# Softmax denominators summed on GpSimd in one buffer, seven PSUM banks, and values multiplied in halves, in an attention and LoRA-mixture layer

## The chip, the cores and the metric

The kernel runs on one core of a Trainium2 chip. The metric is the device time of one execution in microseconds (us); lower is better. All data is float32 unless said otherwise.

## The reference

One transformer layer on `x` of shape 2 × 2048 × 512 (two sequences), in two halves, each with a residual:

```python
x = x + attention(layernorm(x))      # 16 heads of 32, rotary q and k, causal softmax, Wo
x = x + ffn(layernorm(x))            # base linear + bias, and top-2 of 8 LoRA experts of rank 16

# attention, per head
scores = q @ k.T / sqrt(32); scores[above the diagonal] = -inf
attn   = softmax(scores); ctx = attn @ v; out = ctx @ Wo.T

# ffn, per token
probs = softmax(x @ router_w.T + router_b); gate = the two largest, divided by their sum
y     = x @ base_w.T + base_b + 2 * sum over experts of gate[e] * (x @ A[e]) @ B[e]
```

## The kernel before

**Blocks and steps.** The 4096 tokens are cut into eight blocks of 512, four for each sequence: block n is the j-th of its sequence, j = n mod 4. A block has four steps (n, g), one for each group g of four heads, since four heads of 32 fill the 128 partitions. Step (n, g) attends 512 queries to 4j+4 key tiles of 128 keys each. The last four tiles lie on the diagonal; of these, tile 4j+1 and 4j+3 share one buffer, because together they are 512 wide (384 and 128), and tile 4j+2 has 256 columns.

**The two passes over the scores.** `row_maxima` computes scores with the queries on the partitions (`sm`, L367), takes each row's maximum on VectorE (`pm`, L375 and L380) and leaves minus the maximum, split into three bf16 parts, in `max`. `attend` computes the scores again, transposed, with the keys on the partitions (`sc`, L463), adds the shift by a small bf16 matmul (L471), and ScalarE takes the exponential from PSUM into an SBUF buffer `pt` of 128 × 4 × 512 (L485): for one key tile the weights of four heads and 512 queries. On the diagonal GpSimd sets the weights above it to zero (`affine_select`, L494).

**Values and denominators.** `weighted` multiplies the weights of a key tile by its values and adds up in the PSUM bank `av` (L519), four heads side by side. When both tiles of a pair are multiplied, GpSimd adds the second one's weights to the first's in place (L534), two heads at a time, and `summed` later adds the pair's weights over the keys by a matmul with `ones` into the PSUM bank `den` (L545), again four heads side by side. After a step's last pair ScalarE copies `den` to `sum`; its four rows go to DRAM and come back spread over 128 partitions (`few`), VectorE takes the reciprocal, and they go back over DRAM, repeated over 32 partitions each (`sum<-over`). GpSimd then multiplies the context by it (L581). The last step takes the reciprocal directly.

**The order.** TensorE, ScalarE and VectorE run in the order in which the program writes their instructions. GpSimd's and SP's instructions are placed by the scheduler. `side_by_side` interleaves one step's maxima with the former step's weights. It gives out phases: in each, two heads' `sm` and the other two heads' `sc` run side by side on TensorE. Between phases the main loop puts other work:

- `between()` does what is due of `due`: `weighted` two phases after its exponentials, `summed` three after its pair;
- a planner takes projections (`kps`, `qps`, `vps`, L185 and L210) and the stages of the last block but one's second half (`ops`, `mid`, `yps`, L239, L265, L320) from `waiting`, by their times and a credit;
- `ahead()` takes a `summed` one phase early where nothing else was given to a phase.

**Buffers.** The PSUM banks of scores and projections are six, taken in turn (`bank`); `av` and `den` have one each, eight in all. `pt` has four buffers in turn (`PTS`). Before a tile's exponentials `before()` does every entry of `due` that still holds the buffer to be reused. All weights are loaded once, at the start, and stay in SBUF: `wq`, `wk`, `wv`, `wo` and `base_w` are 1 MB each. `wo` is used by `ops` alone and `base_w` by `yps` alone.

Of the kernel before, what the change touches and what calls it, by code (L numbers as in the profile page):

```python
# [9 lines left out]
F32 = mybir.dt.float32  # L10
# [16 lines left out]
LORA_SCALING = 32.0 / 16.0  # L27
THETA = 10000.0
MASKED = -1e30
PTS = 4  # L30
SWAP = [i ^ 1 for i in range(32)]


# [1 line left out]
def preln_attention_moe_lora(  # L35
# [33 lines left out]

    def bank(name, shape=(P, BLK), dtype=F32):  # L70
        banks[0] += 1
        return ps.tile(list(shape), dtype, tag=f"ps{banks[0] % 6}", name=name)


    ident = const.tile([P, P], F32, name="ident")
# [48 lines left out]
    wq = load_weight(wq_t, "wq")  # L124
    first_turn = load_turn(0)
    wv = load_weight(wv_t, "wv")
    wo = load_weight(wo_t, "wo")
    exp_in = load_weight(expert_in, "exp_in")
    bias_sb = const.tile([P, D + E], F32, name="bias_sb")
    nc.sync.dma_start(out=bias_sb, in_=bias.to_broadcast([P, D + E]))  # L130
    base_w = load_weight(base_wt, "base_w")
    exp_out = const.tile([ER, D], F32, name="exp_out")
    nc.sync.dma_start(out=exp_out, in_=expert_out)

    def moments(xt, t, name):

# [90 lines left out]
    def finish(n, ctx_t):  # L227
# [3 lines left out]

        def load(t):
            held["x"].append(load_x(n, t, True))

        def output(t):
            xt = held["x"][t]
            po = bank(f"ops_{n}_{t}")
            for c in range(NC):
                nc.tensor.matmul(  # L239
                    out=po,  # L240
                    lhsT=ctx_t[c][:, bass.ts(t, P)],
                    rhs=wo[:, c, :],
                    start=(c == 0),
                    stop=(c == NC - 1),
                )
            nc.vector.tensor_add(xt, po, xt)
            held["by"].append(moments(xt, t, f"f{n}"))

# [67 lines left out]
        def result(t):  # L316
            xt = held["x"][t]
            po = bank(f"yps_{n}_{t}")
            for c in range(NC):
                nc.tensor.matmul(  # L320
                    out=po,
                    lhsT=held["xn_t"][:, c, bass.ts(t, P)],
                    rhs=base_w[:, c, :],
                    start=(c == 0),
                    stop=False,
                )
# [83 lines left out]
    due = []  # L410
    phase, begun = [0], [0]

    def later(phases, tile, do, early=0):
        due.append((phase[0] + phases, tile, do, early))
        due.sort(key=lambda entry: entry[0])

    def between():

        many = sum(entry[0] <= phase[0] for entry in due)
        many = min(many, 1 + many // 3)  # L420
        for _ in range(many):
            due.pop(0)[2]()
        return many > 0

    def ahead():

        for i, entry in enumerate(due):
            if entry[0] - entry[3] <= phase[0]:
                return due.pop(i)[2]()


    def attend(s):

# [3 lines left out]
        tiles = NT * (j + 1)  # L437
        together = [(kt,) for kt in range(diagonal + 1)]
        together += [(diagonal + 1, diagonal + 3), (diagonal + 2,)]
        pts, index, paired = {}, {}, {}  # L440

        def low(kt):
            return max(kt - diagonal, 0) * P
# [7 lines left out]
        def quad(*kts):  # L451

            all_of = slice(0 if len(kts) > 1 else low(kts[0]), BLK)
            sc = {}

            def take(r):
                sc[r] = bank(f"sc_{n}_{g}_{kts[0]}_{r}")

            def scores(i, r):
                if i < len(kts):  # L460
                    jj, tt = divmod(kts[i], NT)
                    rows = slice(DK * r, DK * r + DK)
# [12 lines left out]

            def weigh(r):
                if kts[0] not in pts:
                    pt = p2.tile(
                        [P, 4, BLK], F32, tag="pt", bufs=PTS, name=f"pt_{n}_{g}_{kts[0]}"
                    )  # L480
                    for kt in kts:
                        index[kt], pts[kt] = begun[0], pt
                    begun[0] += 1
                pt = pts[kts[0]]
                nc.scalar.activation(  # L485
                    pt[:, r, all_of], sc[r][:, all_of], AF.Exp, scale=1.0 / math.sqrt(DK)
                )
                if kts[0] >= diagonal and r % 2:

                    at = all_of.start  # L490
                    on = pt[:, r - 1 : r + 1, at : at + len(kts) * P]
                    if len(kts) > 1:
                        on = on.rearrange("p h (k q) -> p h k q", q=P)
                    nc.gpsimd.affine_select(  # L494
                        out=on, in_=on, compare_op=ALU.is_ge, fill=0.0, base=0,
                        pattern=[[0, 2]] + [[0, len(kts)]] * (len(kts) > 1) + [[1, P]],
                        channel_multiplier=-1,
                    )

            def before():  # L500

                while any(tile <= begun[0] - PTS for _, tile, _, _ in due):
                    due.pop(0)[2]()

            def after():

                oldest = diagonal + 1 if kts[0] == tiles - 2 else kts[0] - kts[0] % 2
                later(2, index[oldest], lambda: weighted(kts))

            return before, take, scores, shift, weigh, after  # L510

        def weighted(kts):
            if kts[0] == 0:
                s["av"] = ps_o.tile([P, BLK], F32, tag="av", name=f"av_{n}_{g}")
            for kt in kts:
                jj, tt = divmod(kt, NT)
                for r in range(4):
                    rows = slice(DK * r, DK * r + DK)
                    nc.tensor.matmul(  # L519
                        out=s["av"][rows, low(kt) :],  # L520
                        lhsT=values[jj][g][:, tt, rows],
                        rhs=pts[kt][:, r, place(kt)],
                        start=(kt == 0),
                        stop=(kt == tiles - 2),
                    )

            for kt in kts:
                kt -= kt % 2
                paired[kt] = paired.get(kt, 0) + 1
                if paired[kt] == 2:  # L530
                    lo = low(kt + 1)
                    for r in (0, 2):
                        some = pts[kt][:, r : r + 2, place(kt, lo)]
                        nc.gpsimd.tensor_add(some, some, pts[kt + 1][:, r : r + 2, place(kt + 1)])  # L534
                    later(3, index[kt], lambda kt=kt: summed(kt), 1)
            if kts[-1] == tiles - 2:
                s["dest"] = wide.tile([P, BLK], F32, tag="ctx", bufs=6, name=f"ctx_{n}_{g}")
                nc.scalar.copy(s["dest"], s["av"])

        def summed(kt):  # L540
            lo = low(kt)
            if kt == 0:
                s["den"] = ps_o.tile([P, BLK], F32, tag="den", name=f"den_{n}_{g}")
            for r in range(4):
                nc.tensor.matmul(  # L545
                    out=s["den"][DK * r : DK * r + DK, lo:],
                    lhsT=ones,
                    rhs=pts[kt][:, r, lo:],
                    start=(kt == 0),
                    stop=(kt == tiles - 2),  # L550
                )
            if kt == tiles - 2:
                total = p2.tile([P, BLK], F32, tag="tmp", bufs=5, name=f"sum_{n}_{g}")
                nc.scalar.copy(total, s["den"])
# [155 lines left out]
    for step in steps + [None]:  # L710
# [18 lines left out]
        for i in range(slots):  # L729
# [3 lines left out]
            for _ in side_by_side(*todo):  # L733
# [14 lines left out]
                while waiting and waiting[0][2] <= phase[0]:  # L748
# [13 lines left out]
                if not given:  # L762
                    ahead()
        late = part(weights, slots - 1, slots)
        if step:
            split()
# [2 lines left out]
        phase[0] += 1  # L769
        between()  # L770
    while due:
        due.pop(0)[2]()
    while aside:
        aside.pop(0)[1]()
    for stage in finish(len(blocks) - 1, contexts[len(blocks) - 1]):
# [52 lines left out]
```

## Time and profile before

| what | us |
|---|---|
| median of three runs | 1982.68 (1980.56 to 1984.05) |
| profiled execution, time | 1982.82 |
| profiled execution, span from first to last instruction | 1981.0 |
| TensorE (PE) busy | 1918.0, 97% of the span |
| GpSimd (POOL) busy | 1008.7, 51% |
| VectorE (DVE) busy | 1018.2, 51% |
| ScalarE (ACT) busy | 768.0, 39% |
| the adds of L534 on GpSimd | 609.9 in 320 instructions |
| `den` matmuls, L545 | 163.3 in 1280 instructions, two for each f32 matmul |
| mean granted TensorE clock | 0.987 |

A row of the costliest groups gives line, engine, operation, result and operands, shape and count; then, behind the first bar, the group's busy time and the mean of one in ns; behind the second, the time for which the engine stood before them and what ended most of it. Matmuls of four heads run side by side, so the busy time of a group is less than count times mean. Blocks are long or short by j; by the first scores of each block's first step the blocks begin at about 68, 177, 388, 669, 1000, 1126, 1365 and 1644, and from 1940 on only the last block's second half is left.

### The profile page before, as it was taken

What the parts mean: (1) busy time and instruction counts of PE and PEld (TensorE: products, weight loads), DVE (VectorE), ACT (ScalarE), POOL (GpSimd) and SP (SyncE); (2) the same over time, 40 slices, a digit from 0 to 9 for tenths busy, and PEclk for the clock granted to TensorE, in tenths of its full rate; (3) what the DMA queues carried; (4) which work ended last, traced back from release to release, by engine and by line L of the source; (5) the groups of instructions that cost most, each with busy time, mean ns of one, the idle gap of its engine ahead of it and who ended that gap; (6) DMA issues with size and microseconds to landing.
All of it is one profiled execution on the core that took longest, in us unless ns stands there. A gap on an engine that the chain in (4) does not pass through costs nothing.

```text
span 1981.0 us, 31399 instructions
## 1 busy us (share of the span) xinstructions
PE 1918.0 (97%) x12256; PEld 731.2 (37%) x12256; DVE 1018.2 (51%) x2760; ACT 768.0 (39%) x1601; POOL 1008.7 (51%) x906
## 2 busy tenths in 40 slices
PE   7999999999999999999999999999999999999997
PEld 3433433333333333333343434333433333333333
DVE  3555555555554655553255546446565555555403
ACT  1323342344433444353532334224434334443451
POOL 3545554455464555355565345435555545553572
PEclk9999999999999999999999999989999999999999
DMA  5000110000100000100000001100011000001000
GB/s 186 23 12 13 32 35 22 7 7 28 60 1 7 7 1 18 48 23 8 10 28 12 28 28 38 49 7 7 2 38 49 1 6 7 1 7 44 6 7 22
DMA packets 34861, 46.33 MB, mean 23 GB/s; under 512 B 12956, under 2 KB 13468, under 8 KB 34712
## 3 DMA queue, kind: packets, MB, share of 16 engines
q1 hardware_dynamic: 34712, 44.32, 7.0%
q8 instruction: 96, 1.57, 0.3%
q14 instruction: 53, 0.43, 0.1%
HBM read 35.40 MB, written 8.90 MB: 22 GB/s over the span
## 4 chain that ended last, share of the span: by engine, by line
PE 83%; POOL 7%; issue 4%; DVE 4%; ACT 1%; DMA 1%; SPq 0%; POOLq 0%; DVEq 0%
PE sm L367 24%; PE av L519 13%; PE den L545 6%; PE ops L239 6%; PE vps L210 6%; PE qps L185 5%; PE kps L185 5%; PE yps L320 5%; PE sc L471 5%; PE sc L463 4%; POOL pt L534 3%; POOL pt L494 2%; PE mid L265 1%; PE yps L327 1%; ACT pt L485 1%
## 5 line engine op out<-in xcount | busy, mean ns | idle before, releaser
L485 ACT ACTIVATE pt<-sc 128x512 f32<-128x512 f32 (+1 forms) x1152 | 595.1, 572 | 950.8 <-PE sc L471 882.0
L534 POOL TENSOR_TENSOR pt<-pt,pt 128x1024 f32<-128x1024 f32 (+2 forms) x320 | 609.9, 1920 | 339.2 <-ACT pt L485 193.6
L463 PE MATMUL sc<-q,k 32*128 32x512 f32 (+3 forms) x2560 | 677.5, 576 | 10.7 <-DVE parts L392 10.1
L367 PE MATMUL sm<-k,q 32*128 32x512 f32 (+3 forms) x2560 | 644.1, 574 | 6.3 <-POOL q L201 3.6
L380 DVE TENSOR_REDUCE pm<-sm 128x1 f32<-128x512 f32 x768 | 490.8, 685 | 286.5 <-PE sm L367 273.6
L367 PEld LDWEIGHTS sm<-k,q 32*128 32x128 f32 x2560 | 221.4, 184 | 375.0 <-issue 148.7
L519 PE MATMUL av<-pt,v 128*32 128x512 f32 (+3 forms) x2560 | 306.0, 550 | 19.1 <-POOL pt L494 14.2
L375 DVE CUSTOM_DVE_ANT_0 sm<-sm,mask 128x128 f32<-128x128 f32 (+3 forms) x512 | 245.8, 512 | 141.8 <-PE sm L367 118.7
L471 PE MATMUL sc<-max,ones_b 3*128 3x512 bf16 (+3 forms) x1280 | 261.2, 346 | 0.0
L463 PEld LDWEIGHTS sc<-q,k 32*128 32x128 f32 x2560 | 233.1, 185 | 51.2 <-issue 24.2
L494 POOL TENSOR_SCALAR_AFFINE_SELECT pt<-pt 128x256 f32<-128x256 f32 (+1 forms) x192 | 93.0, 485 | 154.7 <-ACT pt L485 152.2
L545 PE MATMUL den<-pt,ones 128*32 128x512 f32 (+1 forms) x1280 | 163.3, 569 | 0.0
L519 PEld LDWEIGHTS av<-pt,v 128*32 128x32 f32 x2560 | 57.5, 109 | 201.5 <-issue 142.1
L185 PE MATMUL kps<-xnt_a,wk 128*128 128x512 f32 x256 | 123.3, 626 | 5.0 <-ACT xnt_a L156 4.9
L239 PE MATMUL ops<-wo,ctx 128*128 128x512 f32 x256 | 120.2, 614 | 2.7 <-POOL ctx L581 2.7
L320 PE MATMUL yps<-base_w,xnt_f 128*128 128x512 f32 x256 | 116.9, 599 | 2.6 <-DVE pm L380 1.6
L185 PE MATMUL qps<-xnt_a,wq 128*128 128x512 f32 x256 | 118.3, 605 | 0.0
L210 PE MATMUL vps<-wv,xnt_a 128*128 128x512 f32 x256 | 117.5, 604 | 0.0
L471 PEld LDWEIGHTS <-ones_b 3*128 3x128 bf16 x1280 | 78.3, 94 | 101.0 <-issue 94.5
L200 POOL TENSOR_TENSOR sw_q<-sw_q,sin 128x512 f32<-128x512 f32 x32 | 40.7, 1273 | 112.5 <-DVE sw_q L198 112.5
L200 POOL TENSOR_TENSOR sw_k<-sw_k,sin 128x512 f32<-128x512 f32 x32 | 40.7, 1273 | 109.2 <-DVE sw_k L198 93.8
L581 POOL TENSOR_TENSOR ctx<-ctx,sum 128x512 f32<-128x512 f32 x32 | 40.6, 1268 | 90.1 <-DMA sum<-over 84.8
(85 smaller groups left out, 1246.4 us busy)
## 6 DMA issues: line engine op xcount, KB each, us to landing
xa<-in_x SPq DMA_DIRECT2D x32, 256.0 KB
xf<-in_x SPq DMA_DIRECT2D x32, 256.0 KB
out<-xf SPq DMA_DIRECT2D x32, 256.0 KB
sum<-over SPq DMA_DIRECT2D x124, 64.0 KB
cos<-in_cos SPq DMA_DIRECT2D x8, 256.0 KB
sin<-in_sin SPq DMA_DIRECT2D x8, 256.0 KB
sums<-sum SPq DMA_DIRECT2D x124, 2.0 KB
wk<-in_wk_t SPq DMA_DIRECT2D x1, 1024.0 KB
```

The lines of the kernel that those rows point to most:

```text
L185: nc.tensor.matmul(out=pj, lhsT=w[:, c, bass.ts(g, P)], rhs=held["xn_t"][:, c, :], start=(c == 0), stop=(c == NC - 1),)
L210: nc.tensor.matmul(out=pv, lhsT=held["xn_t"][:, c, bass.ts(t, P)], rhs=wv[:, c, :], start=(c == 0), stop=(c == NC - 1),)
L239: nc.tensor.matmul(out=po, lhsT=ctx_t[c][:, bass.ts(t, P)], rhs=wo[:, c, :], start=(c == 0), stop=(c == NC - 1),)
L367: nc.tensor.matmul(out=sc[r][:, some[i]], lhsT=q[rows, bass.ts(ts[i], P)], rhs=keys[c][rows, : wide_of[i]], start=True, stop=True,)
L375: nc.vector.tensor_tensor_reduce(sc[r][:, here], sc[r][:, here], mask[:, BLK - w :], 1.0, 3.0 * MASKED, ALU.add, ALU.max, pm[:, t, r, c : ...
L380: nc.vector.reduce_max(pm[:, t, r, c : c + 1], sc[r], axis=AX.X)
L463: nc.tensor.matmul(out=sc[r][:, place(kts[i])], lhsT=keys[jj][rows, bass.ts(tt, P)], rhs=q[rows, low(kts[i]) :], start=True, stop=False,)
L471: nc.tensor.matmul(out=sc[r][:, place(kts[i])], lhsT=ones_b[rows, :], rhs=s["max"][rows, low(kts[i]) :], start=False, stop=True,)
L485: nc.scalar.activation(pt[:, r, all_of], sc[r][:, all_of], AF.Exp, scale=1.0 / math.sqrt(DK))
L519: nc.tensor.matmul(out=s["av"][rows, low(kt) :], lhsT=values[jj][g][:, tt, rows], rhs=pts[kt][:, r, place(kt)], start=(kt == 0), stop=(kt ...
L534: nc.gpsimd.tensor_add(some, some, pts[kt + 1][:, r : r + 2, place(kt + 1)])
L545: nc.tensor.matmul(out=s["den"][DK * r : DK * r + DK, lo:], lhsT=ones, rhs=pts[kt][:, r, lo:], start=(kt == 0), stop=(kt == tiles - 2),)
```

## The change

**The sum of weights.** Key tile 0's weights go into a buffer of their own, `acc`, of which there are two. Once its values are multiplied, GpSimd adds the weights of every other tile of the step into it, two heads at a time, in the order in which they come. `summed` then runs once a step: four matmuls with `ones`, into a bank taken in turn. The bank held by `den` is added to the turn, which has seven now. `pt` has three buffers.

**The values.** `weighted` gets its work as two halves: two halves of the columns for a single tile, the two tiles for the pair. Where just one entry is due and no stage of the planner may start by the next phase, `between()` does one half and puts the other at the head of `due`. Else it does a whole tile as before. `ahead()` is gone.

**The weights in SBUF.** `wo` and `base_w` share one buffer, loaded in turn in each block: `wo` with the first load of the block's second half, `base_w` after the last `ops`.

```diff
-PTS = 4
+PTS = 3
-        return ps.tile(list(shape), dtype, tag=f"ps{banks[0] % 6}", name=name)
+        return ps.tile(list(shape), dtype, tag=f"ps{banks[0] % 7}", name=name)
-    wo = load_weight(wo_t, "wo")
-    base_w = load_weight(base_wt, "base_w")
+    def load_in_turn(src, name):
+        w = wide.tile([P, NC, D], F32, tag="w", name=name)
+        nc.sync.dma_start(out=w, in_=src.rearrange("(c p) o -> p c o", p=P))
+        return w
...
         def load(t):
             held["x"].append(load_x(n, t, True))
+            if t == 0:
+                held["w"] = load_in_turn(wo_t, f"wo_{n}")
         def output(t):
...
-                    rhs=wo[:, c, :],
+                    rhs=held["w"][:, c, :],
...
+            if t == NT - 1:
+                held["w"] = load_in_turn(base_wt, f"base_w_{n}")
...
     def between():
         many = sum(entry[0] <= phase[0] for entry in due)
         many = min(many, 1 + many // 3)
-        for _ in range(many):
-            due.pop(0)[2]()
+        spare = any(entry[2] <= phase[0] + 1 for entry in waiting)
+        if many == 1 and not spare:
+            due.pop(0)[2](1)
+        else:
+            for _ in range(many):
+                due.pop(0)[2](2)
         return many > 0
-    def ahead():
...
             def weigh(r):
                 if kts[0] not in pts:
+                    tag, bufs = ("pt", PTS) if kts[0] else ("acc", 2)
                     pt = p2.tile(
-                        [P, 4, BLK], F32, tag="pt", bufs=PTS, name=f"pt_{n}_{g}_{kts[0]}"
+                        [P, 4, BLK], F32, tag=tag, bufs=bufs, name=f"pt_{n}_{g}_{kts[0]}"
                     )
...
+                if kts[0] and r % 2:
+                    ready.extend((kt, r - 1) for kt in kts)
+                    add()
...
             def after():
-                oldest = diagonal + 1 if kts[0] == tiles - 2 else kts[0] - kts[0] % 2
-                later(2, index[oldest], lambda: weighted(kts))
+                if len(kts) == 1:
+                    lo = low(kts[0])
+                    mid = (lo + BLK) // 2
+                    halves = [(kts[0], lo, mid), (kts[0], mid, BLK)]
+                else:
+                    halves = [(kt, low(kt), BLK) for kt in kts]
+                later(2, index[kts[0]], lambda many: weighted(halves, many))
...
-                    for r in (0, 2):
-                        some = pts[kt][:, r : r + 2, place(kt, lo)]
-                        nc.gpsimd.tensor_add(some, some, pts[kt + 1][:, r : r + 2, place(kt + 1)])
-                    later(3, index[kt], lambda kt=kt: summed(kt), 1)
...
+            if kt == 0:
+                s["first"] = True
+                add()
+            if kt == tiles - 2:
                 s["dest"] = wide.tile([P, BLK], F32, tag="ctx", bufs=6, name=f"ctx_{n}_{g}")
                 nc.scalar.copy(s["dest"], s["av"])
+                later(2, 1 << 30, summed)
+        def add():
+            while s["first"] and ready:
+                kt, r = ready.pop(0)
+                some = pts[0][:, r : r + 2, low(kt) :]
+                nc.gpsimd.tensor_add(some, some, pts[kt][:, r : r + 2, place(kt)])
-        def summed(kt):
...
+        def summed(_):
+            den = bank(f"den_{n}_{g}")
             for r in range(4):
                 nc.tensor.matmul(
-                    out=s["den"][DK * r : DK * r + DK, lo:],
...
+                    out=den[DK * r : DK * r + DK, :], lhsT=ones, rhs=pts[0][:, r, :],
+                    start=True, stop=True,
                 )
```

More of the change, by code (lines that the diff above doesn't have):

```diff
@@ L322, in result @@
                     lhsT=held["xn_t"][:, c, bass.ts(t, P)],
-                    rhs=base_w[:, c, :],
+                    rhs=held["w"][:, c, :],
                     start=(c == 0),
@@ L411, in preln_attention_moe_lora, with later @@
     phase, begun = [0], [0]
-    def later(phases, tile, do, early=0):
-        due.append((phase[0] + phases, tile, do, early))
+    def later(phases, tile, do):
+        due.append((phase[0] + phases, tile, do))
         due.sort(key=lambda entry: entry[0])
@@ L420, in between @@
         many = min(many, 1 + many // 3)
-        for _ in range(many):
-            due.pop(0)[2]()
+        spare = any(entry[2] <= phase[0] + 1 for entry in waiting)
[4 more added lines that the diff above has]
+                due.pop(0)[2](2)
         return many > 0
-    def ahead():
-        for i, entry in enumerate(due):
-            if entry[0] - entry[3] <= phase[0]:
-                return due.pop(i)[2]()
     def attend(s):
@@ L439, in attend @@
         together += [(diagonal + 1, diagonal + 3), (diagonal + 2,)]
-        pts, index, paired = {}, {}, {}
+        pts, index, ready = {}, {}, []
+        s["first"], s["av"] = False, None
         def low(kt):
@@ L477, in weigh @@
                 if kts[0] not in pts:
+                    tag, bufs = ("pt", PTS) if kts[0] else ("acc", 2)
                     pt = p2.tile(
-                        [P, 4, BLK], F32, tag="pt", bufs=PTS, name=f"pt_{n}_{g}_{kts[0]}"
+                        [P, 4, BLK], F32, tag=tag, bufs=bufs, name=f"pt_{n}_{g}_{kts[0]}"
                     )
+                    begun[0] += kts[0] > 0
                     for kt in kts:
-                        index[kt], pts[kt] = begun[0], pt
-                    begun[0] += 1
+                        index[kt], pts[kt] = begun[0] if kts[0] else 1 << 30, pt
                 pt = pts[kts[0]]
@@ L498, in weigh, with weighted @@
                     )
+                if kts[0] and r % 2:
+                    ready.extend((kt, r - 1) for kt in kts)
+                    add()
             def before():
-                while any(tile <= begun[0] - PTS for _, tile, _, _ in due):
-                    due.pop(0)[2]()
+                while kts[0] and any(tile <= begun[0] + 1 - PTS for _, tile, _ in due):
+                    due.pop(0)[2](2)
             def after():
-                oldest = diagonal + 1 if kts[0] == tiles - 2 else kts[0] - kts[0] % 2
-                later(2, index[oldest], lambda: weighted(kts))
+                if len(kts) == 1:
[5 more added lines that the diff above has]
+                later(2, index[kts[0]], lambda many: weighted(halves, many))
             return before, take, scores, shift, weigh, after
-        def weighted(kts):
-            if kts[0] == 0:
+        def weighted(halves, many):
+            if s["av"] is None:
                 s["av"] = ps_o.tile([P, BLK], F32, tag="av", name=f"av_{n}_{g}")
-            for kt in kts:
+            whole = len(halves) == many == 2 and halves[0][0] == halves[1][0]
+            now, left = halves[:many], halves[many:]
+            for kt, lo, hi in [(halves[0][0], low(halves[0][0]), BLK)] if whole else now:
                 jj, tt = divmod(kt, NT)
+                at = place(kt).start - low(kt)
                 for r in range(4):
@@ L519, in weighted @@
                     nc.tensor.matmul(
-                        out=s["av"][rows, low(kt) :],
+                        out=s["av"][rows, lo:hi],
                         lhsT=values[jj][g][:, tt, rows],
-                        rhs=pts[kt][:, r, place(kt)],
-                        start=(kt == 0),
-                        stop=(kt == tiles - 2),
-                    )
[L527 to L531, printed above, removed]
-                    for r in (0, 2):
-                        some = pts[kt][:, r : r + 2, place(kt, lo)]
-                        nc.gpsimd.tensor_add(some, some, pts[kt + 1][:, r : r + 2, place(kt + 1)])
-                    later(3, index[kt], lambda kt=kt: summed(kt), 1)
@@ L536, in weighted @@
-            if kts[-1] == tiles - 2:
+                        rhs=pts[kt][:, r, at + lo : at + hi],
+                        start=(kt == 0 and lo == 0),
+                        stop=(kt == tiles - 2 and hi == BLK),
+                    )
+            if left:
+                due.insert(0, (0, index[left[0][0]], lambda many: weighted(left, many)))
+                return
+            kt = halves[-1][0]
+            if kt == 0:
+                s["first"] = True
+                add()
+            if kt == tiles - 2:
@@ L537, in weighted @@
                 s["dest"] = wide.tile([P, BLK], F32, tag="ctx", bufs=6, name=f"ctx_{n}_{g}")
                 nc.scalar.copy(s["dest"], s["av"])
-        def summed(kt):
-            lo = low(kt)
-            if kt == 0:
-                s["den"] = ps_o.tile([P, BLK], F32, tag="den", name=f"den_{n}_{g}")
+                later(2, 1 << 30, summed)
[4 more added lines that the diff above has]
+                nc.gpsimd.tensor_add(some, some, pts[kt][:, r : r + 2, place(kt)])
@@ L544, in summed @@
+        def summed(_):
+            den = bank(f"den_{n}_{g}")
             for r in range(4):
                 nc.tensor.matmul(
-                    out=s["den"][DK * r : DK * r + DK, lo:],
[L547 to L550, printed above, removed]
+                    out=den[DK * r : DK * r + DK, :], lhsT=ones, rhs=pts[0][:, r, :],
+                    start=True, stop=True,
                 )
-            if kt == tiles - 2:
+            if True:
@@ L553, in summed @@
                 total = p2.tile([P, BLK], F32, tag="tmp", bufs=5, name=f"sum_{n}_{g}")
-                nc.scalar.copy(total, s["den"])
+                nc.scalar.copy(total, den)
                 if (n, g) == steps[-1]:
@@ L761, in preln_attention_moe_lora @@
                     given = given or us > 0.0
-                if not given:
-                    ahead()
         late = part(weights, slots - 1, slots)
@@ L771, in preln_attention_moe_lora @@
     while due:
-        due.pop(0)[2]()
+        due.pop(0)[2](2)
     while aside:
```

## The prediction

> **What bounds the kernel now.** I read the page first, then the groups by form, then TensorE's timeline, then the engine windows by block. On the page (busy time; chain; costly groups):
>
> ```profile
> PE 1918.0 (97%) x12256; PEld 731.2 (37%) x12256; DVE 1018.2 (51%) x2760; ACT 768.0 (39%) x1601; POOL 1008.7 (51%) x906
> ...
> PE 83%; POOL 7%; issue 4%; DVE 4%; ACT 1%; DMA 1%; SPq 0%; POOLq 0%; DVEq 0%
> ...
> L534 POOL TENSOR_TENSOR pt<-pt,pt 128x1024 f32<-128x1024 f32 (+2 forms) x320 | 609.9, 1920 | 339.2 <-ACT pt L485 193.6
> ```
>
> TensorE carries the chain, GpSimd works half the time. 97% doesn't mean that every TensorE us is needed. The timeline of a stretch of block 3 gives the price of work put between two phases (a phase: two heads' maxima scores and the other two heads' shifted scores, eight f32 passes side by side):
>
> ```profile
> 865.81 0.69 PE L367 MATMUL sm<-k,q 32*128 32x512 f32 x1
> ...
> 867.10 1.06 PE L545 MATMUL den<-pt,ones 128*32 128x512 f32 x8
> 868.09 0.69 PE L367 MATMUL sm<-k,q 32*128 32x512 f32 x1
> ...
> 869.38 1.06 PE L519 MATMUL av<-pt,v 128*32 128x512 f32 x8
> 870.38 0.69 PE L367 MATMUL sm<-k,q 32*128 32x512 f32 x1
> ...
> 873.68 1.06 PE L519 MATMUL av<-pt,v 128*32 128x512 f32 x8
> 874.67 0.69 PE L367 MATMUL sm<-k,q 32*128 32x512 f32 x1
> ```
>
> 865.81 to 868.09 and on to 870.38: a phase with one group (`den` or `av`, 512 columns, four heads) takes 2.28; the group starts 1.29 after its phase and holds TensorE 1.00. From 870.38 to 874.67 there are two phases and one group, 4.29, where 1.29+1.29+1.00 = 3.58 would do: a phase with nothing behind it loses about 0.7, because its successor lacks PSUM banks. Phases with a 256-column `den` take 1.86, so that group costs 0.57; a projection adds 3.63.
>
> GpSimd's prices, from the groups by form, and the blocks' windows (block 2, block 3, block 7, last projections):
>
> ```profile
> L534 POOL TENSOR_TENSOR pt<-pt,pt 128x1024 f32<-128x1024 f32 x192 | 448.9, 2354 | 279.9 <-ACT pt L485 193.6 <-PE av L519 86.0
> L534 POOL TENSOR_TENSOR pt<-pt,pt 128x768 f32<-128x768 f32 x64 | 116.0, 1812 | 6.8 <-PE av L519 1.5
> L534 POOL TENSOR_TENSOR pt<-pt,pt 128x256 f32<-128x256 f32 x64 | 45.0, 725 | 52.5 <-PE av L519 52.5
> ```
>
> ```profile
> 388.40:668.60 280.20, 276.03 (x1824) 102.08 (x1824) 157.27 (x392) 113.30 (x232) 144.62 (x121) 1.00 0.06 18
> 668.60:999.50 330.90, 325.41 (x2188) 115.67 (x2185) 157.90 (x401) 144.02 (x291) 180.51 (x139) 0.99 0.06 17
> ...
> 1644.30:1940.00 295.70, 286.58 (x2017) 99.52 (x2014) 136.52 (x321) 132.64 (x261) 162.38 (x116) 0.98 0.04 12
> 1940.00:1981.00 41.00, 33.67 (x114) 17.42 (x112) 14.08 (x61) 8.03 (x20) 8.82 (x15) 0.99 0.07 26
> ```
>
> Columns: stretch, length, then busy time of PE, PEld, DVE, ACT, POOL. The reader should see how much room POOL has in each block: 180.5 of 330.9 in block 3.
>
> [...]
>
> **The change, part by part.**
>
> *TensorE.* Removed: 128 `den` groups of 512 columns and 32 of 256: 128×1.00 + 32×0.57 = 146. Added: one 512 group a step, 32×1.00 = 32. By the order of instructions, `av` goes from 1280 to 1584 matmuls: 76 groups more, about 72 of them a 512 group cut in two (2×0.57−1.00 = 0.14), 10. Net −104. Per step of a block with j earlier blocks: 2j+0.2; per block of four steps 1, 9, 17, 25 for j = 0 to 3.
>
> *GpSimd.* The adds of 1024 elements double, 192 to 384; 64 of 768 stay; 64 of 512 are new at 1.27 (the rotary row of that size); 64 of 256 stay: 904+116+81+46 = 1147 for 610, so +537, total 1546. Per block +10, +48, +86, +123. Against the room: block 2: 144.6+86 = 231 of 280.2−17 = 263 (88%). Block 3: 180.5+123 = 304 of 330.9−25 = 306 (99%). Block 7: 162.4+123 = 285 of 295.7−25 = 271 (105%). A key tile costs GpSimd 2×2.354 = 4.71, TensorE two phases and its values, 2×1.29+1.1 = 3.7, where no projection lies between. So **at j = 3 GpSimd becomes the bound**; three `pt` buffers let ScalarE run at most three tiles ahead, and then exponentials, banks and scores stop.
>
> *The new wait.* `den` now waits for a step's last add. The last tiles leave 2×(1.81+0.73) + 2×1.27 + 4×0.5 = 9.6 of adds and selects, while four short phases pass before `den`, about 8 to 9. With a backlog TensorE stands 2 to 7 a step at j = 2 and 3; behind it stand the next step's scores and so all engines. The context multiply (L581) waits for the sums' DMA on GpSimd's queue, 84.8 in 25 waits, 3.4 each; its adds now queue behind it. At j = 0 and 1 GpSimd's load leaves room and I take 1.5 a block at j = 1.
>
> *Block by block.* 0: −1; 4: −1. 1: −9+1.5 = −7.5; 5 the same. 2 and 6: −17 + 7 (the waits of four steps) = −10 each. Block 3: GpSimd's 304 plus 4.5 idle a step (the 3.4, and the start, where the first tile's values must be multiplied before it may be added into) = 322, −9. Block 7: 285+18, plus 8 because after the last scores no other work covers the last adds: 311, +15. Sum −31.
>
> *Banks.* Seven for six: 31 bare full phases lose 0.7 each, 22; it may give back 0 to 22; I take 5, since 34 remain bare. The halves' phases: 0 to 0.18 lost in about 135 (a 256-column `av` phase took 2.04, a `den` one 1.86), 0 to 24; I take 0 because of the seventh bank.
>
> *Weights loaded in turn.* 14 more loads of 1 MB on SP's queue, past the sums' transfers. The first slice of the page moves 186 GB/s: estimate 5.6 each. By the order and the prices above, 23 us or more of TensorE work lie between the last `ops` and the first `yps` of a block, 10 for `wo` of block 3, and in the tail the profile has 10 between them: hidden, 0; without that cover 14×5.6 = 79. A load waiting for the last `ops` holds up `few` and `sum` behind it, 0 to a few us; 0 taken. Dropping `ahead` moves summing only: its work is gone.
>
> Span: 1981.0−31−5 = 1945; outside it 1.8 (1982.82 profiled), so 1946.8; the median of the runs, 1982.68, is the same as the profiled one. I say 1946.
>
> **The rivals.**
> A. GpSimd keeps up: no wait at `den`, banks give back all: −104−12+8 → 1875. For it: the adds of different tiles need no answer from anyone. Against: 99% and 105%.
> B. GpSimd starves while it is the bound (slower). Now it waits in order, per step, 3.4 on the sums' DMA and (112.5+93.8)/32 = 6.4 on VectorE's shuffles for the rotary multiply: 9.8. My forecast has 4.5 in eight steps at j = 3. Each us more costs 8; from 9 us a step the gain of 36 is gone. At 11 to 12: 1946+8×7 = 2002. For it: the queue is in order and placed by estimate. Against: a backlogged queue finds those inputs ready.
> C. The loads are not covered: half of 79, 1946+40 = 1986; unlikely by the distances above.
> D. It doesn't do what it says: excluded by the order of instructions, `den` falls from 640 to 128 matmuls.
>
> **Numbers.** About 0.2% (4 us) is what a measurement can tell from no change. Forecast 0.52 (faster), A 0.17, B 0.24 with C 0.03 in it, around zero 0.07 between. Faster 0.70, same 0.05, slower 0.25. Range: the forecast with its bounds (waits 2 to 7, banks, halves) 1915 to 1975; reaching into A and B: 1890 to 2000.
>
> **Right or wrong, seen in the profile after.** POOL near 1546 busy with 1024-element adds still about 2.35; `den` near 35 busy; POOL over 90% busy in blocks 3 and 7, which gain nothing or lose, while blocks 1, 2, 5, 6 get shorter by 7 to 10; TensorE waiting for POOL at `den`; ACT `pt` waiting for POOL at j = 3. It would be wrong if POOL is idle over 9 a step there (B), if blocks 3 and 7 shorten by 25 (A), or if `yps` or `ops` wait for DMA (C).

## The result, and the profile after

The changed kernel takes **2046.24 us**, the median of four runs (2031.23 to 2048.55), against 1981.85 of the kernel before, measured beside it: a ratio of **1.031, 95% interval 1.026 to 1.036**. It is slower, where the forecast was 1946 and faster. The profiled execution took 2047.29, its span is 2045.6, 64.6 more than before.

The page of the changed kernel: busy time by engine, the granted clock in 40 slices, the chain that ended last, and three of the costliest groups.

```profile
PE 1881.6 (92%) x11840; PEld 731.9 (36%) x11840; DVE 1016.0 (50%) x2760; ACT 767.1 (38%) x1601; POOL 1529.8 (75%) x1162
...
PEclk9999999899999999798799998999999989898869
...
PE 67%; POOL 19%; issue 8%; DVE 3%; DMA 1%; ACT 1%; SPq 0%; POOLq 0%; DVEq 0%; ACTq 0%
...
L563 POOL TENSOR_TENSOR pt<-pt,pt 128x1024 f32<-128x1024 f32 (+3 forms) x576 | 1136.8, 1990 | 173.2 <-ACT pt L494 140.3
...
L539 PE MATMUL av<-pt,v 128*32 128x512 f32 (+3 forms) x3168 | 345.6, 513 | 108.1 <-POOL pt L503 107.8
...
L503 POOL TENSOR_SCALAR_AFFINE_SELECT pt<-pt 128x256 f32<-128x256 f32 (+1 forms) x192 | 93.1, 485 | 58.2 <-ACT pt L494 58.2
```

TensorE is busy 36 us less than before and yet the span is longer: its share fell from 97% to 92%. Behind a group's last bar stands how long its engine stood before it, and behind the arrow what it stood for most: `av` stood 107.8 us for L503, and L503 is neither an add nor a sum. It is the **select** that zeroes the weights above the diagonal. The clock row has slices of 7 and 8, and the mean clock fell from 0.987 to 0.929. Before, the row read:

```profile
PEclk9999999999999999999999999989999999999999
```

The waits of the changed kernel (who, for whom: us in total, times, the longest):

```profile
PEld av L539 <- POOL pt L503: 146.1, 65, 7.8
...
PE av L539 <- POOL pt L503: 107.8, 52, 7.6
ACT pt L494 <- POOL pt L563: 59.4, 22, 3.9
...
PEld den L568 <- POOL pt L563: 1.1, 1, 1.1
```

The second of these has its counterpart in the kernel before, where `av` is L519 and the select L494:

```profile
PE av L519 <- POOL pt L494: 14.2, 28, 1.3
```

(The first line above is the weight load of the same stands.) The wait that the forecast had named, `den` for the last add, is the last line: 1.1 us. One of the longest stands, in the timeline (start, duration, engine, line; in brackets how long the engine stood and for whom):

```profile
1898.30 2.06 ACT L494 ACTIVATE pt<-sc 128x512 f32<-128x512 f32 x4 [2.55 <-POOL pt L563]
...
1902.84 4.65 POOL L563 TENSOR_TENSOR pt<-pt,pt 128x1024 f32<-128x1024 f32 x2
...
1907.43 0.41 POOL L503 TENSOR_SCALAR_AFFINE_SELECT pt<-pt 128x256 f32<-128x256 f32 x1
1907.93 2.34 POOL L563 TENSOR_TENSOR pt<-pt,pt 128x1024 f32<-128x1024 f32 x1
1910.22 0.41 POOL L503 TENSOR_SCALAR_AFFINE_SELECT pt<-pt 128x256 f32<-128x256 f32 x1
...
1910.68 1.08 PE L539 MATMUL av<-pt,v 128*32 128x256 f32 x8 [7.58 <-POOL pt L503]
```

The exponentials of this tile end at 1900.4, but GpSimd works through adds without a gap. The select of two heads gets its turn at 1907.43, one more add goes next, and only at 1910.22 comes the select of the other two heads, 0.41 long. TensorE has been standing for 7.58 by then. It can't go round it, since the scores of the next phases are behind this `av` on its own queue: they begin at 1911.69.

The stretches between the ends of the blocks (each block taken from the last `ctx` copy of the former one to its own) tell where the 64.6 lie. The last column has the stands of `av` for selects in the changed kernel:

| block | before | after | forecast of the difference | difference | stands of `av` for selects |
|---|---|---|---|---|---|
| 0, with the start | 168.8 | 167.8 | −1 | −1.0 | 8.4 |
| 1 | 210.9 | 218.5 | −7.5 | +7.6 | 11.6 |
| 2 | 280.2 | 283.2 | −10 | +3.0 | 10.2 |
| 3 | 330.9 | 347.4 | −9 | +16.5 | 23.3 |
| 4 | 130.2 | 120.1 | −1 | −10.1 | 0.7 |
| 5 | 235.5 | 246.1 | −7.5 | +10.6 | 13.8 |
| 6 | 279.1 | 283.2 | −10 | +4.1 | 10.6 |
| 7 | 293.3 | 327.3 | +15, with the end | +34.0 | 29.1 |
| the end | 52.2 | 52.0 | | −0.2 | 0 |

All blocks but 0 and 4 miss the forecast by 13 to 26, not blocks 3 and 7 alone, and all of these have stands of 10 us or more. The engines' busy time in blocks 3 and 7 of the changed kernel (stretch, length, then PE, PEld, DVE, ACT, POOL, the granted clock, the DMA share, GB/s):

```profile
669.60:1016.90 347.30, 317.14 (x2136) 114.00 (x2140) 157.90 (x393) 146.30 (x296) 301.85 (x192) 0.90 0.07 22
...
1666.30:1993.60 327.30, 292.59 (x2122) 105.00 (x2122) 136.78 (x322) 136.02 (x270) 284.59 (x170) 0.87 0.06 17
```

GpSimd's 302 and 285 are what the forecast said (304 and 285). It idles 45 and 43 beside them, 11 a step. Over the whole kernel its adds wait mostly for exponentials (140.3 in their line above), and the exponentials wait for TensorE's scores (934.3, `pt` L494 for `sc` L479), so TensorE and GpSimd wait for each other in turn.

### The profile page after: what moved, and what is told of

It is laid out like the page before. It is cut to its first block, busy times and chain, and to the rows that moved or that the text cites. A ratio compares the mean times of both kernels' runs of the same rounds, so it can differ in the third digit from the quotient of the medians.

```text
span 2045.6 us, 31136 instructions
## 1 busy us (share of the span) xinstructions
PE 1881.6 (92%) x11840; PEld 731.9 (36%) x11840; DVE 1016.0 (50%) x2760; ACT 767.1 (38%) x1601; POOL 1529.8 (75%) x1162
## 4 chain that ended last, share of the span: by engine, by line
PE 67%; POOL 19%; issue 8%; DVE 3%; DMA 1%; ACT 1%; SPq 0%; POOLq 0%; DVEq 0%; ACTq 0%
PE sm L375 20%; POOL pt L563 13%; PE av L539 10%; PE qps L189 5%; PE yps L328 5%; PE vps L214 5%; PE kps L189 5%; PE ops L245 5%; PE sc L479 4%; PE sc L471 2%; POOL pt L503 2%; PE den L568 2%; PE yps L335 1%; POOL k L205 1%; PE mid L273 1%
## 5 line engine op out<-in xcount | busy, mean ns | idle before, releaser
L563 POOL TENSOR_TENSOR pt<-pt,pt 128x1024 f32<-128x1024 f32 (+3 forms) x576 | 1136.8, 1990 | 173.2 <-ACT pt L494 140.3
L494 ACT ACTIVATE pt<-sc 128x512 f32<-128x512 f32 (+1 forms) x1152 | 594.2, 572 | 1006.3 <-PE sc L479 934.3
L471 PE MATMUL sc<-q,k 32*128 32x512 f32 (+3 forms) x2560 | 703.1, 618 | 14.3 <-DVE pm L383 5.4
L375 PE MATMUL sm<-k,q 32*128 32x512 f32 (+3 forms) x2560 | 655.7, 609 | 7.5 <-POOL q L205 3.6
L539 PE MATMUL av<-pt,v 128*32 128x512 f32 (+3 forms) x3168 | 345.6, 513 | 108.1 <-POOL pt L503 107.8
L479 PE MATMUL sc<-max,ones_b 3*128 3x512 bf16 (+3 forms) x1280 | 261.8, 365 | 0.0
L539 PEld LDWEIGHTS av<-pt,v 128*32 128x32 f32 x3168 | 71.5, 115 | 356.6 <-issue 171.8
L503 POOL TENSOR_SCALAR_AFFINE_SELECT pt<-pt 128x256 f32<-128x256 f32 (+1 forms) x192 | 93.1, 485 | 58.2 <-ACT pt L494 58.2
L479 PEld LDWEIGHTS <-ones_b 3*128 3x128 bf16 x1280 | 80.7, 99 | 107.3 <-issue 99.5
L245 PEld LDWEIGHTS ops<-wo,ctx 128*128 128x128 f32 x256 | 47.3, 194 | 71.2 <-issue 62.5
L189 PEld LDWEIGHTS qps<-xnt_a,wq 128*128 128x128 f32 x256 | 47.4, 195 | 70.6 <-issue 56.9
```

The lines of the kernel that those rows point to most:

```text
L189: nc.tensor.matmul(out=pj, lhsT=w[:, c, bass.ts(g, P)], rhs=held["xn_t"][:, c, :], start=(c == 0), stop=(c == NC - 1),)
L245: nc.tensor.matmul(out=po, lhsT=ctx_t[c][:, bass.ts(t, P)], rhs=held["w"][:, c, :], start=(c == 0), stop=(c == NC - 1),)
L375: nc.tensor.matmul(out=sc[r][:, some[i]], lhsT=q[rows, bass.ts(ts[i], P)], rhs=keys[c][rows, : wide_of[i]], start=True, stop=True,)
L471: nc.tensor.matmul(out=sc[r][:, place(kts[i])], lhsT=keys[jj][rows, bass.ts(tt, P)], rhs=q[rows, low(kts[i]) :], start=True, stop=False,)
L479: nc.tensor.matmul(out=sc[r][:, place(kts[i])], lhsT=ones_b[rows, :], rhs=s["max"][rows, low(kts[i]) :], start=False, stop=True,)
L494: nc.scalar.activation(pt[:, r, all_of], sc[r][:, all_of], AF.Exp, scale=1.0 / math.sqrt(DK))
```

## The experiments

The theory after the result: **the selects**. A diagonal tile's `av` needs its select, the select stands behind adds in GpSimd's queue (in the timeline above one runs 7.1 us after its exponentials have ended), and TensorE in its own order stands behind that `av` (7.58 there). The rivals: GpSimd's amount of work alone (its pace), the loads in turn, and the halves. (No run changes the number of `pt` buffers in the changed kernel alone.)

**The selects left out (e1), and the control (e2).** In the kernel after and in the kernel before:

```diff
-                if kts[0] >= diagonal and r % 2:
+                if False:
```

> The changed kernel with GpSimd's selects on the diagonal tiles left out (weights above the diagonal stay in the sums; the output is not the reference's). Theory W (a diagonal tile's values wait on TensorE for its select, which stands in GpSimd's queue behind adds; each such stand also costs granted clock afterwards): the 49 stands before av (107 us) vanish, granted clock 0.975 or more, time 1890 to 1930. Rival T (GpSimd is simply too slow: adds and pt buffers bound the long steps): only the selects' own 93 us leave GpSimd, most of it not on the path, time 2000 or more. Rival L (the 1 MB loads or the halved values cost): time 2020 or more.

> The kernel before, with the same selects left out (output not the reference's): the control of the run before. Theory W: they stand at eight places for 11 us in all here, so 1965 to 1982. Rival T and L: no difference, 1975 to 1985.

Measured: e1 1897.6, ratio to before 0.958 (0.956 to 0.959); e2 1973.2, 0.995 (0.993 to 0.997). The page of e1, busy time and chain:

```profile
PE 1820.1 (96%) x11840; PEld 727.1 (38%) x11840; DVE 1013.3 (53%) x2760; ACT 766.1 (40%) x1601; POOL 1439.9 (76%) x970
...
PE 84%; issue 6%; POOL 6%; DVE 2%; ACT 1%; DMA 0%; POOLq 0%; DVEq 0%; ACTq 0%
```

The selects are 93 us of work on GpSimd. Leaving them out gives 149 us after the change and 9 before it. They are not dear in themselves; what costs is what waits for them. POOL's share of the chain falls from 19% to 6%. The spans of after and e1 differ by 150.5, and that splits in two: TensorE's time not busy falls from 164.0 to 75.0, by 89, and the same 11840 matmuls are busy 61.5 less, at a higher clock (0.978 for 0.929).

The wait that the prediction named, `den` for the last add, shows up in e1, but in two steps alone:

```profile
PE den L568 <- POOL pt L563: 12.7, 2, 8.7
```

**The mask on another engine (e3, e9).** e3 puts the zeroes in on VectorE, by a multiply with a triangle of zeroes and ones; e9 does it on TensorE, by adding a triangle of −1e30 to the scores ahead of the exponential.

```diff
-                    nc.gpsimd.affine_select(
...
+                    nc.vector.tensor_mul(on, on, by)
```

```diff
-                        rhs=s["max"][rows, low(kts[i]) :], start=False, stop=True,
+                        rhs=s["max"][rows, low(kts[i]) :], start=False, stop=kts[i] < diagonal,
...
+                    for h in (r - 1, r) if kts[i] >= diagonal and r % 2 else ():
+                        at = place(kts[i]).start
+                        nc.tensor.matmul(
+                            out=sc[h][:, at : at + P], lhsT=ident_b, rhs=above,
+                            start=False, stop=True,
+                        )
```

> The changed kernel with the selects done by VectorE as a multiply by a 0/1 triangle instead of by GpSimd. Theory W: no queue of adds ahead of the mask any more, so av no longer stands; VectorE gains about 93 us of work beside its 1016; clock 0.97 or more; 1890 to 1945, faster than the kernel before. Rival T: 2000 or more, ACT pt waiting for POOL grows. If VectorE becomes the holder (its queue waits for exponentials): 1950 to 1990.

> The changed kernel with the diagonal masked on TensorE: a bf16 matmul of the identity with a triangle of -1e30 adds to the scores of the diagonal tiles ahead of the exponential (512 matmuls of 128 columns), and no select. Theory W: as without selects, 1897.6, plus 512 matmuls at about 0.1, 51: 1925 to 1955, faster than the kernel before; no stand before av. Rival T: 1990 or more.

Measured: e3 1999.8, 1.010 (1.006 to 1.013); e9 **1939.3, 0.980 (0.978 to 0.981)**. e3 is better than the changed kernel, but stays 102 above e1, just under the range of rival T and in neither of its other two; T's mark isn't there, since ScalarE's wait for GpSimd's adds fell from 59.4 to 48.2. Its multiply, by form, and the stands that it made (waits):

```profile
L512 DVE TENSOR_TENSOR pt<-pt,tri 128x256 f32<-128x256 f32 x128 | 138.4, 1084 | 42.2 <-ACT pt L500 38.5 <-POOL pt L568 2.1
```

```profile
PE av L544 <- DVE pt L512: 33.5, 39, 3.5
...
PE sc L477 <- DVE pm L389: 29.9, 23, 8.1
```

The multiply of 128x256 took 1084 ns in the mean, the one of 128x512 1209, where VectorE's multiply of 128x512 for the rotary k took 674 in the same run; and GpSimd's adds of 128x256 took 879, for 723 in the changed kernel. Why these take longer is not shown. VectorE then is late with the maxima (`pm`), for whose PSUM banks the scores stand (29.9, for 5.4 in the changed kernel). So e3 moves part of the wait and doesn't remove it. e9 asks nothing of GpSimd or VectorE within the steps; its 512 matmuls cost 42 us against e1, 0.08 each, and no `av` stands for POOL. This version beats both kernels.

**GpSimd's pace, the bank, the halves (e8, e7, e6),** each beside e1 without selects, so that their sizes show uncovered:

```diff
-                    ready.extend((kt, r - 1) for kt in kts)
+                    ready.extend((kt, r - 1) for kt in kts if r == 1)
```

```diff
-        return ps.tile(list(shape), dtype, tag=f"ps{banks[0] % 7}", name=name)
+        return ps.tile(list(shape), dtype, tag=f"ps{banks[0] % 6}", name=name)
```

```diff
-            due.pop(0)[2](1)
+            due.pop(0)[2](2)
```

> The changed kernel without selects and with the adds of heads 0 and 1 alone, so half of them (output not the reference's): GpSimd falls from 1440 to about 870 busy. Against 1897.6: theory W says GpSimd's pace costs little once no value waits for it, 1870 to 1893 (pt waits of ScalarE and the tail go); rival T says it still sets the long steps, 1860 or less.

> The changed kernel without selects (output not the reference's) and with six banks in turn instead of seven, the eighth bank left unused. Against 1897.6: 10 to 35 slower if the seventh bank takes stands away from the half-filled phases; within 5 if not.

> The changed kernel without selects (output not the reference's) and with every single tile's values multiplied whole, never in halves. Against the same kernel with halves (1897.6): if the halves fill gaps as meant, 10 to 25 slower, 1908 to 1922; if the seventh bank already fills them, within 5; if the halves cost more than they fill (76 groups more, 10 us), 5 to 12 faster.

Measured: e8 1832.7, 0.924 (0.923 to 0.926); e7 1945.2, 0.981 (0.979 to 0.983); e6 1910.8, 0.963 (0.962 to 0.965). Busy time of e8:

```profile
PE 1784.5 (98%) x11840; PEld 715.7 (39%) x11840; DVE 1013.5 (55%) x2760; ACT 766.5 (42%) x1601; POOL 885.0 (48%) x682
```

Half of the adds gone gives 65 more: GpSimd's pace does cost, also with the selects away, and more than the theory of the selects allowed; the rival had this size right. As in e1, part of the gain is TensorE's busy time: 35.6 less, at a clock of 0.992 for 0.978. Of the 65, block 7 has 33.5 (289.1 in e1, 255.6 in e8), block 3 has 8.0, and blocks 0, 1 and 5 have nothing.

Blocks 1 and 5 part the two theories. Once the selects are away, taking 555 us of adds from GpSimd doesn't shorten these blocks at all, so its pace doesn't bound them; but leaving out the selects had shortened them by 20.0 and 23.7 (from 218.5 to 198.5 and from 246.1 to 222.3). In blocks 3 and 7, where e1 gained 41 and 38, both count.

The seventh bank is worth 47.5, more than expected, the halves 13.

**The loads (e5).** The kernel before, with `wo` and `base_w` loaded in turn as after the change:

```diff
-    wo = load_weight(wo_t, "wo")
-    base_w = load_weight(base_wt, "base_w")
...
+                held["w"] = load_in_turn(wo_t, f"wo_{n}")
...
+                held["w"] = load_in_turn(base_wt, f"base_w_{n}")
```

> The kernel before with one part of the change alone: wo and base_w loaded in turn into one buffer, 14 loads of 1 MB more. Theory W: the loads are covered, 1978 to 1987. Rival L: they hold ops, yps or the sums' transfers, 1990 or more.

Measured: 1980.6, 0.999 (0.998 to 1.000). The loads are out as a cause; in the changed kernel, too, no `ops` or `yps` waits for a DMA.

**More GpSimd work without the rest of the change (e10).** The kernel before with each add issued twice:

```diff
-                        nc.gpsimd.tensor_add(some, some, pts[kt + 1][:, r : r + 2, place(kt + 1)])
+                        for _ in range(2):
+                            nc.gpsimd.tensor_add(some, some, pts[kt + 1][:, r : r + 2, place(kt + 1)])
```

> The kernel before with each of its adds issued twice (output not the reference's): GpSimd does about as many adds as in the changed kernel, TensorE's work stays. Theory W: the selects, late behind the adds, hold av and the clock falls: 2030 to 2130, clock 0.96 or less, ten stands or more before av. If GpSimd's added work alone were harmless while it is under 80% busy: 1978 to 2000.

Measured: 2141.2, 1.081 (1.080 to 1.083), 11 above the range of the theory. Its waits:

```profile
PE av L519 <- POOL pt L494: 78.8, 40, 5.4
...
PE den L546 <- POOL pt L535: 27.0, 25, 2.2
```

With POOL busy 1611.5 the old kernel gets the same stands at the same place, with neither the new sum, nor three `pt` buffers, nor halves. The load on GpSimd's queue is enough for these stands. The two lines make 106 of the 161 us that this kernel lost; the rest, likely the lower clock (0.956) and GpSimd's pace, is parted by no run.

**The stands filled (e4).** The changed kernel, with four matmuls nobody uses (3.63 us) put before `av` at eleven of the long stands:

```diff
+            if (n, g, halves[0][0]) in WARM and len(halves) == 2:
+                fill = bank(f"fill_{n}_{g}")
+                for c in range(NC):
+                    nc.tensor.matmul(
+                        out=fill, lhsT=wq[:, c, :P], rhs=wq[:, c, :],
...
```

> The changed kernel with eleven projections' worth of unused matmuls (3.63 us each) put where TensorE stood 3.7 to 7.6 us before a diagonal tile's values. They lie inside the stand, so they cost nothing by themselves. If stands also cost clock (half speed for 3.4 to 20 us after each): clock up from 0.929 to 0.945 or more, time 2005 to 2035. If only the stand itself counts: 2040 to 2060, clock figures aside.

Measured: 2037.5, 1.028 (1.025 to 1.031), against 1.031 of the changed kernel: no clear difference, and the time lies between the two expectations. 40 us of work were added, and the stands of `av` for selects fell from 107.8 to 77.2, so some 31 of the 40 lay in stands. The clock rose from 0.929 to 0.945, just the mark that was set for stands that cost clock, and the time at half speed (in the changed kernel, spells of 3.41 to 27.31 us in its clock records, one at the end shorter) fell from 291 to 226 us. How much time such filling could save stays open.

**The order on GpSimd's queue (e11, e12, e13).** e11 was to issue a step's diagonal adds behind its last select, with GpSimd's queue written out in program order:

```diff
-    ctx.enter_context(tc.manual_schedule(engines={et.PE, et.Activation, et.DVE}))
+    ctx.enter_context(tc.manual_schedule(engines={et.PE, et.Activation, et.DVE, et.Pool}))
...
-                    add()
+                    if kts[0] < diagonal or kts[0] == tiles - 2 and r == 3:
+                        add()
```

> The changed kernel, whole, with GpSimd's queue in the program's order and the adds of the diagonal tiles issued behind the step's last select; only adds of earlier tiles stand ahead of the first select. Theory W: stands before av fall from 107 to 30 to 60, 1950 to 2010. If only the sum of GpSimd's work counts: 2035 to 2060.

Measured: 2189.4, 1.105 (1.104 to 1.107), the worst of all. As run, one add of 512 elements a step (heads 0 and 1 of the last tile) was left out. The timeline shows why the expectation failed:

```profile
639.15 10.98 POOL L564 TENSOR_TENSOR pt<-pt,pt 128x1024 f32<-128x1024 f32 x7
...
650.08 0.41 POOL L503 TENSOR_SCALAR_AFFINE_SELECT pt<-pt 128x256 f32<-128x256 f32 x1
...
650.54 0.20 PEld L540 LDWEIGHTS av<-pt,v 128*32 128x32 f32 x8 [9.26 <-POOL pt L503]
650.54 1.08 PE L540 MATMUL av<-pt,v 128*32 128x256 f32 x8 [8.43 <-POOL pt L503]
...
651.55 1.22 PE L375 MATMUL sm<-k,q 32*128 32x512 f32 x1
```

Heads 2 and 3 come first in this phase, so the condition released seven adds, 11 us together, ahead of the last select and not behind it. Unmeant, it is the strongest case for the mechanism: TensorE stood 209.3 us for selects, 6.5 a step, and here it stood 8.43 for one select of 0.41. The last line shows what comes after: a matmul that took 0.69 in the lines of the kernel before takes 1.22. The mean clock of this run was 0.902.

e12 has only the order by hand. e13 is e12 with the diagonal adds truly behind the sixth select:

```diff
-            while s["first"] and ready:
+            while s["first"] and ready and (ready[0][0] < diagonal or s["selects"] == 6):
```

> The changed kernel with GpSimd's queue alone put in program order by hand, as it is for the three other engines; every add and every select is kept where the program writes it. Run e11 changed two things at once: this order, and putting the adds of the diagonal groups behind the last select of the step. If it was the order by hand that cost its 143 us over the changed kernel, this one is at 2120 to 2190 us with TensorE's av waiting for the selects for 160 us or more. If putting the adds behind the selects was what cost, this one stands near the changed kernel, 2030 to 2070 us, with av waiting for about 108 us.

> Run e12 (GpSimd's queue in program order) with the adds of a step's diagonal tiles held back until the sixth and last select of the step is issued: the same instructions, another order on GpSimd's queue. If the place of the selects in the queue is what costs, TensorE's av waits less for them: the 109 us of e12 fall to 20 to 60 us (the first selects of a step still stand behind adds of the tiles before the diagonal), no part of the gain is given back in full, and the time is 1960 to 2010 us. If it is the amount of work on GpSimd and not its order, the lump of some 10 us of adds behind the last select delays den, the context multiply and the next step's buffers as much, and the time is 2025 to 2070 us with the waits moved to den and to the exponentials.

Measured: e12 2043.8, 1.031 (1.029 to 1.033), as the changed kernel: the order by hand costs nothing. e13 2094.6, 1.057 (1.054 to 1.061). Waits of e12:

```profile
PE av L539 <- POOL pt L503: 109.0, 51, 7.7
POOL pt L503 <- ACT pt L494: 55.4, 23, 6.6
```

Waits of e13:

```profile
POOL pt L503 <- ACT pt L494: 197.0, 99, 6.9
...
PE den L570 <- POOL pt L565: 110.8, 26, 8.7
...
PE av L541 <- POOL pt L503: 43.1, 28, 7.7
```

`av` stands 43 for selects instead of 109, inside what the theory of the place in the queue expected. But the waits moved, as the rival had it, and by more than it said, so both expectations of the time were too low: `den` now stands 111 for the last add, and GpSimd idles 197 for the exponentials of selects (55 in e12), because it has no add to do between them. Amount and place belong together: at the end of a step GpSimd owes TensorE some 10 us of work, and whichever piece TensorE needs first, it waits for all that stands ahead of it. The runs that helped took work or the deadline from GpSimd (e1, e8, e9, in part e3).

## Why the prediction was wrong, point by point

**The step that failed is "The new wait".** It counted the selects as work for GpSimd ("9.6 of adds and selects") and asked who waits for the last add. It didn't ask who waits for each *other* instruction in that queue. `av` of a diagonal tile waits for selects of 0.4 to 0.6, and now these stand behind adds of 2.35 each: up to 7.6 in one stand. Priced at nothing, this costs 150 (e1). The wait at `den`, 2 to 7 a step at j = 2 and 3, was named in its place and was wrong too: it comes to 1.1 in the changed kernel and to 12.7 in e1, without selects, in the last steps of blocks 3 and 7 alone. It becomes large, 111 us or 3.5 a step, only in e13, where the adds are held back behind the selects.

**The lower clock had no term.** The stands took 108; the same matmuls ran 61.5 longer against e1. The clock records of the changed kernel have 38 spells at half speed, 291 us in all, against 12 and 52 before, each but the shortest a multiple of 3.41. So a stand seems to be paid for once while it lasts and again after it; that is the author's estimate, from the 108 and the 61.5. That the spells come with the stands is seen in the runs: 291 us at half speed in the changed kernel, 226 with eleven stands filled (e4), 83 without selects (e1). How much time the lower clock alone costs, apart from the stands, is not shown.

**Banks: the term was mis-sized.** 5 taken out of 0 to 22; e7 measures 47.5. The 0.7 behind bare phases was read from full phases alone; blocks 0 and 4, where all tiles lie on the diagonal, have 16 of the 47.5 (e7 against e1), so the short phases seem to lack banks too. Phases beside projections are not parted from them by any run.

**What held.** POOL's busy time (1546 said, 1529.8), the adds' 2.35 (2352 ns), `den` (35 said, 36.1), loads at 0 (e5). The halves, 0 to 24 lost, gain 13. GpSimd's pace and its waits, the difference between −104 and −31, were 73; e8 has 65, most of it in block 7 (40 said there, 33.5 and 5 in the end) and block 3 (16 said, 8). TensorE's −104: e8 is 149 below the kernel before; 47.5 of that are the bank's and 9 the selects' own, so about 93 are left, the halves' 13 among them, if the parts simply add up. With the bank and the pace as measured the forecast's own sum is 1981 − 104 − 47 + 65 = 1895, and e1's span is 1895.1. That they meet so closely is partly luck, since the selects' 9 and the halves' 13 are not in the sum.

**The rivals.** A (1875) needed a GpSimd that keeps up (and takes 12 for the banks, where the prediction's own term allows 22); C is out by e5. B had the sign, but its 2002 is 44 short, and it had not the cause: its mark, over 9 idle a step at j = 3, is there (11), though GpSimd's wait for the sums' DMA, which B blamed, fell from 84.8 to 30.3. An idle engine is a poor mark for one cause, since any stand elsewhere makes it idle. Wrong too was the sign "blocks 1, 2, 5, 6 get shorter by 7 to 10": each has as many diagonal tiles as blocks 3 and 7, and each got longer.

## What to carry to other kernels

Before bulk work goes onto a queue that runs in order, as GpSimd's does in these traces (a select 7.1 us after its exponentials, behind adds), list every instruction in that queue that another engine waits for, and charge each of them with the new work that can stand ahead of it. Here it was the short ones with an early deadline (selects of 0.4 us) that cost, not the last one. Ask, too, which engine could do the piece that has the deadline: the same mask as 512 small matmuls on TensorE cost 42 us where the select in GpSimd's queue cost 150. A stand of TensorE counts for more than its length where the clock falls with it: here, beside 108 us of stands for selects, the same matmuls were busy 61.5 longer than in e1, at a clock of 0.929 for 0.978.

## What the runs showed of the hardware

- In the changed kernel 37 of the 38 half-speed spells are whole multiples of 3.41 us, up to 8 of them (27.31 us). One runs from 1906.5, within the stand of 7.58 that ends at 1910.68, to 1916.8. Ahead of another, which begins at 520.7, the longest stand of TensorE in 20 us was 1.36: that of `av` for a select, up to 519.08.
- The multiply of 128x256 on VectorE with two SBUF inputs (e3) took 1084 ns in the mean, the one of 128x512 1209. The rotary multiply of 128x512 took 674 in the same run.
- The identity-times-triangle matmul of 128 columns in bf16, appended to a group already open in PSUM, came to 0.08 us each in the time of the whole kernel (1939.3 in e9, 1897.6 in e1, 512 matmuls).
